# One score product ahead of a wait, and a reordered first batch, in a two-layer graph-attention kernel

## The chip, the cores and the metric

The kernel runs on one core of a Trainium2 chip. The metric is the device time of one execution in microseconds (us), and the number compared is the median of several executions. Before the change three executions took 3313.91, 3315.76 and 3318.42 us, so the median is 3315.76 us.

## The reference

The input is `x` with shape (16, 1024, 256) and an integer mask `adj` with shape (16, 1024, 1024). Two graph-attention layers follow each other, and each adds its result to `x`:

```
h = relu(layernorm(x))
# layer 0
n   = layernorm(h) * gamma1 + beta1               # 8 heads of width 32; q = k = v = n
h   = h + softmax(mask(n n^T / sqrt(32))) n
x   = x + h + gelu(layernorm(h)*gamma2+beta2 @ W1 + b1) @ W2 + b2
# layer 1
f   = relu(layernorm(x))
g   = f W
e   = leaky_relu(g a_1 (row) + g a_2 (column) + (g a_12) g^T, 0.2)
att = softmax(where(adj > 0, e, -9e15))
x   = x + elu(f W_1 + (att f) W_2)
```

The mask is symmetric. Batches do not depend on each other.

## The kernel before, in words

Everything is computed by `fast_path`; a second routine, `general_path`, is only entered when a check at the end says that the quick one is not accurate enough, and it does not run on these inputs. One batch has 1024 rows, which are cut into 8 tiles of 128 (`NT`), 4 chunks of 256 (`NCH`) or 2 halves of 512 (`NQH`).

The program is written out once by Python loops, without a loop on the chip. Six generators produce the pieces of work: `stream_a` (attention of layer 0), `stream_b` (the MLP and layer 1, called "rest"), `stream_p` (`prepare`, the second normalization), `stream_c` (`prologue`: load and normalize the next batch), `stream_m` (masks), `stream_s` (weights). Each yields a place on a common scale on which batch b's attention fills the stretch from b to b+1. The generator with the lowest place goes next. So the numbers in the `stream_...` functions decide the order in which instructions are issued. At the end the program adds an ordering dependency between successive instructions of each engine, so that every engine works strictly through its own list. A small list of deferred steps (`defer`) puts a step behind others by an estimated time; that too is only an order.

**Layer 0.** `attention` goes through units (half of the queries, group of four heads, key tile). In a unit, TensorE makes 4 score tiles (`s`, L1062), VectorE adds the mask to them (L1081), ScalarE takes the exponential (L1088), and in the unit after that TensorE weighs the values (`o`, L1183). In batch 0 there are 32 units; there TensorE adds the mask to half of the score tiles itself, by a product with an identity (`s<-mk,ident`, L574), and VectorE to the other half. In later batches VectorE adds every mask, and 8 of the 32 units are replaced by reading back weights from the other half (`mirror`, `weigh_mirrored`). The score tiles have one buffer each (`sc0`, `sc1`).

**The rest.** While batch b+1 is in its attention, TensorE also does the MLP (`ph`, `po`) and layer 1 of batch b. Layer 1 starts with a stage that this case is much about. `turn1(c)` turns the normalized features of chunk c into `fT` (`ptf`, L1423, copied out by ScalarE at L1426). `project_half(qh, oc)` makes half of `uT` (`puT`, copied out by ScalarE at L1438). `some_values(t, ...)` makes one tile `pg` of values each, copied to `gw` at L1453 by ScalarE for an even t and VectorE for an odd t. `some_weights(c, i)` makes the logits `lg` of chunk c against key tiles 2i and 2i+1; VectorE reads them twice (L1471), applies the leaky ReLU (L1476), and ScalarE takes the exponential (L1477). `ptf`, `puT`, `pg`, `lg`, `ph`, `po`, `pa`, `pf`, `ptk` and `ptos` share three PSUM buffers of one pool (`ps_tile`, `psm`); a product waits until an earlier tenant of its buffer has been read.

**The first batch.** `prologue` for b = 0 is written out by hand. Chunks 0 and 1 are normalized (`nrm`, L761), turned straight away (`turn_normed`, with gamma and beta applied by ScalarE during the copy to `kT`), and gamma and beta are applied to the values `va` by GpSimd (L863, L864). Chunks 2 and 3 go another way: GpSimd applies gamma and beta first (L844, L845), then `turn` transposes the result (`ptk`, L871).

**Masks.** `turn_masks(b, qh)` fetches the int32 mask in halves of a tile (two buffers, `adjp`), converts it on VectorE (`mq<-adj`, L594) and turns it by a transposing DMA. It runs in 5 pieces. `compare_masks(b, qh)` checks that the mask is symmetric: GpSimd subtracts (`odd`, L975), and the result is collected by ScalarE (a square with a sum, L985) for the first half and by VectorE (a maximum, L987) for the second. The tiles `odd` lie in a pool of six buffers.

Of the kernel before, what the change touches and what calls it, by code (L numbers as in the profile page):

```python
# [495 lines left out]
def fast_path(  # L496
# [307 lines left out]
    def prologue(b, st):  # L804
        h = hs[b] = [hp.tile([P, TPH, D], F32, tag=f"h{qh}", name=f"h{qh}_{b}") for qh in range(NQH)]


        va = st["va"] = vp.tile([P, NT, D], F32, tag="va", name=f"va_{b}")
        kT = st["kT"] = vp.tile([P, NG, N], F32, tag="kT", name=f"kT_{b}")
        stats = {}  # L810

        def load(i):
            ts = slice(i % 2 * TPC, (i % 2 + 1) * TPC)
            nc.sync.dma_start(
                h[i // 2][:, ts, :], x[b, i * CW : (i + 1) * CW, :].rearrange("(p r) d -> p r d", r=TPC)
            )

        def measure(i, which):
            stats[which, i] = norm_stats(
                [h[i // 2][:, i % 2 * TPC + j, :] for j in range(TPC)], f"{which}{b}_{i}"  # L820
            )

        def rectify(i):
            mv, rs = stats["a", i]
            nm = offset(mv, rs, f"{b}_{i}")
            for j in range(TPC):
                t = i * TPC + j
                nc.scalar.activation(
                    h[t // TPH][:, t % TPH, :],
                    h[t // TPH][:, t % TPH, :],  # L830
                    AF.Relu,
                    bias=nm[:, j : j + 1], scale=rs[:, j : j + 1]
                )

        def value(i):
            mv, rs = stats["b", i]
            for j in range(TPC):
                t = i * TPC + j
                nrm = tmpp.tile([P, D], F32, tag="w1", bufs=6, name=f"nrm_{b}_{t}")
                normalize(nrm, h[t // TPH][:, t % TPH, :], mv, rs, j)  # L840
                if b == 0 and i < 2:
                    normed[t] = nrm
                    continue
                nc.gpsimd.tensor_mul(nrm, nrm, g1)  # L844
                nc.gpsimd.tensor_add(va[:, t, :], nrm, be1)  # L845

        normed = {}

        def turn_normed(i):
            clock[0] += 0.5  # L850
            pt = ps_tile([P, NG, CW], f"ptk_{b}_{i}")
            for g in range(NG):
                for j in range(TPC):
                    nc.tensor.transpose(
                        pt[:, g, j * P : (j + 1) * P], normed[i * TPC + j][:, g * P : (g + 1) * P], ident
                    )
            for g in range(NG):
                nc.scalar.activation(
                    kT[:, g, i * CW : (i + 1) * CW], pt[:, g, :], AF.Identity, bias=be1c[:, g : g + 1], scale=g1c[:, g : g + 1]
                )  # L860
            for j in range(TPC):
                t = i * TPC + j
                nc.gpsimd.tensor_mul(va[:, t, :], normed[t], g1)  # L863
                nc.gpsimd.tensor_add(va[:, t, :], va[:, t, :], be1)  # L864

        def turn(i):
            clock[0] += 0.5
            pt = ps_tile([P, NG, CW], f"ptk_{b}_{i}")
            for g in range(NG):
                for j in range(TPC):  # L870
                    nc.tensor.transpose(  # L871
                        pt[:, g, j * P : (j + 1) * P], va[:, i * TPC + j, g * P : (g + 1) * P], ident
                    )
            nc.scalar.copy(kT[:, :, i * CW : (i + 1) * CW], pt)

        steps = [
            load,
            lambda i: None,
            lambda i: measure(i, "a"),
            rectify,  # L880
            lambda i: measure(i, "b"),
            value,
            lambda i: None,
            lambda i: turns.append((1, lambda: turn(i))),
        ]
        if b == 0:

            tiles = [midp.tile([P, 2, N], I32, tag=f"mid{i}", name=f"adj_0_{i}") for i in range(2)]
            adjs = [tiles[t // 2][:, t % 2] for t in range(TPH)]
            mqs = st["mq", 0] = mqp.tile([P, TPH, N], FP8, tag="mq", name="mq_0_0")  # L890
            m = st[0] = mkp.tile([P, NT // 2, QW, 2], FP8, tag="mk", name="mk_0_0")
            pairs = m.rearrange("p m q r -> p m (q r)").bitcast(BF16)

            def fetch(t):
                nc.sync.dma_start(adjs[t], rows(adj, 0, t))

            def convert(t):
                nc.vector.tensor_scalar(
                    mqs[:, t], adjs[t], 0.0, NEG8, op0=ALU.is_le, op1=ALU.mult, saturate=False
                )  # L900
                nc.sync.dma_start_transpose(pairs[:, :, t * P : (t + 1) * P], mqs[:, t].bitcast(BF16))

            load(0)
            load(1)
            for t in range(TPH):
                fetch(t)
                if t == 0:
                    for tile, src in first_rows:
                        nc.sync.dma_start(tile, src)
            load(2)  # L910
            load(3)
            measure(0, "a")
            measure(1, "a")
            rectify(0)
            rectify(1)
            measure(0, "b")
            measure(1, "b")
            value(0)
            turn_normed(0)
            convert(0)  # L920
            value(1)
            turn_normed(1)
            convert(1)
            convert(2)
            convert(3)
            yield
            for f in (lambda i: measure(i, "a"), rectify):
                for i in (2, 3):
                    f(i)
            yield  # L930
            measure(2, "b")
            value(2)
            yield
            measure(3, "b")
            value(3)
            yield
            for i in (2, 3):
                turns.append((1, lambda i=i: turn(i)))
                yield
            return  # L940
        for k in range(NCH + len(steps) - 1):
            for n in reversed(range(len(steps))):
                if 0 <= k - n < NCH:
                    steps[n](k - n)
                    yield
# [21 lines left out]
    def compare_masks(b, qh, st):  # L967

        for half in range(qh + 1):
            for i in range(TPH):  # L970
# [10 lines left out]
                n = (b * 3 + qh + half) * TPH + i  # L981

                def collect(odd=odd, n=n):
                    if qh == 0:
                        nc.scalar.activation(odd, odd, AF.Square, accum_out=uneven[:, n : n + 1])  # L985
                    else:
                        nc.vector.tensor_reduce(  # L987
                            uneven[:, n : n + 1], odd, axis=mybir.AxisListType.X, op=ALU.max, apply_absolute_value=True
                        )
# [332 lines left out]
    def rest(b, st, tails):  # L1322
# [262 lines left out]
        yield from some_values(2, 3)  # L1585
        if b == B - 1:
            ask(turn1, 3)
        yield from wait_for(turn1, 2)
        yield from some_values(4, 5)
        yield from some_weights(0, 0, 1)  # L1590
        yield from wait_for(turn1, 3)
        yield from project_half(1, 0)
        yield from project_half(1, 1)
        yield from some_values(6, 7)

# [38 lines left out]
        yield from spread(close_attention(), 4, B, B + .1)  # L1634

    def starts(b):
        return b + 0.99

    def stream_b():
        for b in range(B):  # L1640
# [22 lines left out]

    def stream_p():
        for b in range(B):
            place = starts(b) - 0.08
            yield place
            for c in range(2):
                while finished.get((b, 0), 0) < NG:
# [9 lines left out]
    def stream_c():  # L1679
        for b in range(B):  # L1680
            if b == 0:
                yield -0.6
                for place, _ in zip((0.005, 0.032, 0.034, 0.07, 0.10, 0.13), prologue(b, states[b])):
                    yield place
            else:
                yield from spread(prologue(b, states[b]), 32, b - 0.660, b - 0.150)

    def stream_m():
        for b in range(B):
            if b:  # L1690
                start, end = (b - 0.28, b - 0.10) if b == 1 else (b - 0.73, b - 0.60)
                yield from spread(turn_masks(b, 0, states[b]), 5, start, end)
                yield from spread(compare_masks(b, 0, states[b]), TPH, end + 0.05, end + 0.14)
                yield from spread(turn_masks(b, 1, states[b]), 5, b + 0.02, b + 0.16)
                yield from spread(compare_masks(b, 1, states[b]), 2 * TPH, b + 0.17, b + 0.26)
            else:
                yield from spread(compare_masks(b, 0, states[b]), TPH, b + 0.02, b + 0.2)
                yield from spread(turn_masks(b, 1, states[b]), 5, b + 0.23, b + 0.43)
                yield from spread(compare_masks(b, 1, states[b]), 2 * TPH, b + 0.52, b + 0.7)

    def stream_s():
        yield -0.3
# [82 lines left out]
```

## Time and profile before

| what | value |
|---|---|
| median of three executions | 3315.76 us |
| the profiled execution | 3309.42 us |
| its span | 3307.5 us |
| TensorE (PE) busy | 3216.8 us, 97% |
| VectorE (DVE) busy | 2575.4 us, 78% |
| ScalarE (ACT) busy | 2125.9 us, 64% |
| GpSimd (POOL) busy | 1660.3 us, 50% |
| DMA | 438.43 MB, mean 133 GB/s |

"Busy" counts the time in which an engine has an instruction in work; a busy TensorE is not TensorE at its peak. The profile also gives the share of its full clock that TensorE was granted in any stretch, the waits (who waited for whom, in total, how often, the longest), and a timeline of each engine. SP is the engine that issues the DMAs.

### The profile page before, as it was taken

What the parts mean: (1) busy time and instruction counts of PE and PEld (TensorE: products, weight loads), DVE (VectorE), ACT (ScalarE), POOL (GpSimd) and SP (SyncE); (2) the same over time, 40 slices, a digit from 0 to 9 for tenths busy, and PEclk for the clock granted to TensorE, in tenths of its full rate; (3) what the DMA queues carried; (4) which work ended last, traced back from release to release, by engine and by line L of the source; (5) the groups of instructions that cost most, each with busy time, mean ns of one, the idle gap of its engine ahead of it and who ended that gap; (6) DMA issues with size and microseconds to landing.
All of it is one profiled execution on the core that took longest, in us unless ns stands there. A gap on an engine that the chain in (4) does not pass through costs nothing. (4 is left out here: it accounts for less than half of the span.)

```text
span 3307.5 us, 115199 instructions
## 1 busy us (share of the span) xinstructions
PE 3216.8 (97%) x48642; PEld 1598.1 (48%) x48642; DVE 2575.4 (78%) x4568; ACT 2125.9 (64%) x5130; POOL 1660.3 (50%) x2397
## 2 busy tenths in 40 slices
PE   7799999999999999999999999999999999999998
PEld 2244445444454544445444454444545444454477
DVE  5688787888878888787888888888788787877734
ACT  6675665757667576675766657576675766757452
POOL 3565562735537365463645637365372654636120
PEclk9999999999999999999999999999999999999999
DMA  5264665646556465655646656465564746554410
GB/s 139 65 151 117 153 133 142 150 122 161 132 150 140 131 159 123 153 131 144 158 112 162 133 142 151 121 161 127 149 141 127 166 114 158 129 148 107 125 58 15
DMA packets 787789, 438.43 MB, mean 133 GB/s; under 512 B 178880, under 2 KB 738368, under 8 KB 787264
## 3 DMA queue, kind: packets, MB, share of 16 engines
q1 hardware_dynamic: 787264, 430.98, 53.4%
q8 instruction: 385, 6.31, 0.8%
q14 instruction: 140, 1.15, 0.1%
HBM read 250.75 MB, written 163.32 MB: 125 GB/s over the span
## 5 line engine op out<-in xcount | busy, mean ns | idle before, releaser
L1088 ACT ACTIVATE e<-e 128x512 f32<-128x512 f32 x1504 | 928.0, 618 | 502.0 <-DVE e L1081 498.0
L1081 DVE TENSOR_TENSOR e<-s,mk 128x1024 f32<-128x1024 f32 x748 | 878.2, 1214 | 127.3 <-PE s L1062 114.5
L574 PE MATMUL ph<-yT,w 128*32 128x256 f32 x7808 | 462.9, 382 | 15.1 <-DVE x L1104 6.0
L1183 PE MATMUL o<-e,va 128*32 128x512 f32 x3136 | 452.8, 611 | 7.9 <-ACT e L1088 7.9
L1062 PE MATMUL s<-kT 32*64 32x512 f32 x6272 | 455.6, 618 | 3.9 <-DVE e L1081 3.0
L574 PE MATMUL lg<-fT,uT 128*32 128x256 f32 x7680 | 450.1, 379 | 0.0
L574 PE MATMUL pa<-gw,e 128*32 128x258 f32 x7584 | 446.0, 380 | 0.0
L574 PE MATMUL po<-w,hid 128*32 128x256 f32 x7680 | 434.8, 379 | 0.4 <-ACT hid L1382 0.4
L574 PEld LDWEIGHTS ph<-yT,w 128*32 128x32 f32 x7808 | 269.7, 110 | 205.4 <-issue 28.2
L574 PEld LDWEIGHTS po<-w,hid 128*32 128x32 f32 x7680 | 251.9, 110 | 201.8 <-issue 43.3
L574 PEld LDWEIGHTS lg<-fT,uT 128*32 128x32 f32 x7680 | 248.6, 110 | 197.9 <-issue 27.2
L574 PEld LDWEIGHTS pa<-gw,e 128*32 128x32 f32 x7584 | 246.1, 110 | 185.4 <-issue 22.1
L1117 POOL TENSOR_TENSOR part<-part,x 128x512 f32<-128x512 f32 x240 | 310.9, 1295 | 18.8
L1104 DVE STREAM_TRANSPOSE x<-e 128x1024 f32<-128x1024 f32 x240 | 290.7, 1226 | 33.2 <-ACT e L1088 27.2
L1088 ACT ACTIVATION_READ_ACCUMULATOR e<-e 128x1 f32 x1504 | 281.3, 187 | 0.0
L1471 DVE SCALAR_TENSOR_TENSOR e<-lg,gw,mk 128x256 f32<-128x256 f32 x512 | 222.1, 475 | 69.9 <-PE lg L574 60.9
L1477 ACT ACTIVATE e<-e,shift 128x512 f32<-128x512 f32 x256 | 183.1, 716 | 137.1 <-DVE e L1476 125.5
L844 POOL TENSOR_TENSOR nrm<-nrm,g 128x256 f32<-128x256 f32 x124 | 97.1, 783 | 307.3 <-DVE nrm L761 307.3
L1183 PEld LDWEIGHTS o<-e,va 128*32 128x32 f32 x3136 | 69.3, 108 | 351.9 <-issue 212.0
L1378 ACT ACTIVATE hid<-ph,b1c 128x256 f32<-128x256 f32 x512 | 202.2, 464 | 57.2 <-PE ph L574 42.0
L975 POOL TENSOR_TENSOR odd<-mk,mq 128x512 bf16<-128x512 fp8e5 x192 | 219.4, 1161 | 0.0
L1117 POOL TENSOR_TENSOR part<-x 128x512 f32<-128x512 f32 x120 | 155.8, 1298 | 114.8 <-DVE x L1104 114.7
(158 smaller groups left out, 4396.6 us busy)
## 6 DMA issues: line engine op xcount, KB each, us to landing
blocks<-x SPq DMA_DIRECT2D x480, 256.0 KB, 4.7
em<-blocks SPq DMA_DIRECT2D x240, 512.0 KB, 4.2
adj<-in_adj_dram SPq DMA_DIRECT2D x248, 256.0 KB, 3.7
h<-in_x_dram SPq DMA_DIRECT2D x64, 256.0 KB, 4.4
xb<-in_x_dram SPq DMA_DIRECT2D x128, 128.0 KB, 3.2
turned<-yT SPq DMA_DIRECT2D x64, 256.0 KB, 3.3
yT<-turned SPq DMA_DIRECT2D x256, 64.0 KB, 2.0
out_dram<-z SPq DMA_DIRECT2D x128, 128.0 KB, 3.9
```

Of the source, the lines that this page charges most:

```text
L574: nc.tensor.matmul(out[c : c + HD], lhsT[:, c : c + HD], rhs, start=start, stop=stop)
L844: nc.gpsimd.tensor_mul(nrm, nrm, g1)
L975: nc.gpsimd.tensor_tensor(odd.rearrange("p (u v x) -> p u v x", u=2, v=2), key.rearrange("p (u v x) -> p u v x", u=2, v=2), query.rearrang ...
L1062: nc.tensor.matmul(sc[j // 2][c : c + P // 2, j % 2, :], kT[r, g, kt * P + c : kt * P + c + P // 2], kT[r, g, qs], start=j >= by_pe, stop= ...
L1081: nc.vector.tensor_tensor(e, masked, mask.unsqueeze(1).to_broadcast([P, 2, QW]), op=ALU.add)
L1088: nc.scalar.activation(e[:, j], masked[:, j], AF.Exp, scale=SCALE, accum_out=sums[kt // TPH, g][:, n, kt % TPH, qh : qh + 1],)
L1104: nc.vector.transpose(x[:, :, 2 * i : 2 * i + 2, :].rearrange("p c h j -> p h c j"), es[i].rearrange("p h (c i) -> p h c i", i=HD),)
L1117: add = lambda out, p, q: nc.gpsimd.tensor_tensor(out, p, q, op=ALU.add)
L1183: nc.tensor.matmul(o[j * HD : (j + 1) * HD, :], va[:, kt, (g * GH + j) * HD : (g * GH + j + 1) * HD], es[j // 2][:, j % 2, :], start=first ...
L1378: nc.scalar.activation(hid[:, f0 + i, :], ph[:, i, :], AF.Identity, bias=b1c[:, f0 + i : f0 + i + 1])
L1471: nc.vector.scalar_tensor_tensor(e[:, j, :], lg[:, j, :], gw[:, kt, D : D + 1], st[c // 2][:, kt // 2, qs, kt % 2], op0=ALU.add, op1=ALU.add,)
L1477: ready = defer(2.5, lambda: nc.scalar.activation(e, e, AF.Exp, bias=shift))
```

## The change

There are five edits.

1. In layer 1 of every batch, the logits of chunk 0 against key tiles 0 and 1 are made ahead of `wait_for(turn1, 2)` and values 4 and 5, and those against key tiles 2 and 3 between the two halves of the second projection.
2. In batch 0, chunks 2 and 3 are normalized as chunks 0 and 1 are: `nrm` is turned directly, ScalarE applies gamma and beta in two activations for each chunk, and GpSimd makes `va` from `nrm` in a step of its own (`scale_values`), outside the transposition. The steps of both chunks stand in another order.
3. The collecting step of the symmetry check goes from ScalarE to VectorE for the first half of the masks in batches 0 and 1.
4. Places in `stream_m`: in batch 0, four comparisons begin later and eight stand in the stretch 0.45 to 0.54 where it was 0.52 to 0.70; both halves of batch 1's masks are fetched and converted earlier, all within batch 0's attention.
5. The MLP of batch 0 starts at 1.03 instead of 0.99, `prepare` keeps its place.

```diff
@@ prologue
-                if b == 0 and i < 2:
+                if b == 0:
                     normed[t] = nrm
                     continue
@@ turn_normed
+        def scale_values(i):
             for j in range(TPC):
                 t = i * TPC + j
                 nc.gpsimd.tensor_mul(va[:, t, :], normed[t], g1)
                 nc.gpsimd.tensor_add(va[:, t, :], va[:, t, :], be1)
@@ prologue, b == 0
             value(1)
             turn_normed(1)
-            convert(1)
-            convert(2)
-            convert(3)
+            for t in range(1, TPH):
+                convert(t)
+            scale_values(0)
+            scale_values(1)
             yield
-            for f in (lambda i: measure(i, "a"), rectify):
-                for i in (2, 3):
-                    f(i)
+            for i in range(2, NCH):
+                measure(i, "a")
             yield
-            measure(2, "b")
-            value(2)
+            for i in range(2, NCH):
+                rectify(i)
+            for i in range(2, NCH):
+                measure(i, "b")
+            for i in range(2, NCH):
+                value(i)
             yield
-            measure(3, "b")
-            value(3)
+            turns.append((1, lambda: turn_normed(2)))
+            scale_values(2)
             yield
-            for i in (2, 3):
-                turns.append((1, lambda i=i: turn(i)))
-                yield
+            turns.append((1, lambda: turn_normed(3)))
+            scale_values(3)
             return
@@ compare_masks
-                    if qh == 0:
+                    if qh == 0 and b > 1:
                         nc.scalar.activation(odd, odd, AF.Square, accum_out=uneven[:, n : n + 1])
@@ rest
+        yield from some_weights(0, 0)
         yield from wait_for(turn1, 2)
         yield from some_values(4, 5)
-        yield from some_weights(0, 0, 1)
         yield from wait_for(turn1, 3)
         yield from project_half(1, 0)
+        yield from some_weights(0, 1)
         yield from project_half(1, 1)
         yield from some_values(6, 7)
@@ starts, stream_p
-        return b + 0.99
+        return b + (0.99 if b else 1.03)
-            place = starts(b) - 0.08
+            place = b + 0.91
@@ stream_c
-                for place, _ in zip((0.005, 0.032, 0.034, 0.07, 0.10, 0.13), prologue(b, states[b])):
+                for place, _ in zip((0.005, 0.032, 0.07, 0.10, 0.13), prologue(b, states[b])):
@@ stream_m
-                start, end = (b - 0.28, b - 0.10) if b == 1 else (b - 0.73, b - 0.60)
+                start, end = (b - 0.44, b - 0.30) if b == 1 else (b - 0.73, b - 0.60)
                 ...
-                yield from spread(turn_masks(b, 1, states[b]), 5, b + 0.02, b + 0.16)
+                start, end = (b - 0.16, b - 0.03) if b == 1 else (b + 0.02, b + 0.16)
+                yield from spread(turn_masks(b, 1, states[b]), 5, start, end)
                 ...
-                yield from spread(compare_masks(b, 0, states[b]), TPH, b + 0.02, b + 0.2)
+                yield from spread(compare_masks(b, 0, states[b]), TPH, b + 0.10, b + 0.20)
                 yield from spread(turn_masks(b, 1, states[b]), 5, b + 0.23, b + 0.43)
-                yield from spread(compare_masks(b, 1, states[b]), 2 * TPH, b + 0.52, b + 0.7)
+                yield from spread(compare_masks(b, 1, states[b]), 2 * TPH, b + 0.45, b + 0.54)
```

## The prediction

> **What bounds the kernel now.** I read the page first: the table of engines, then the slices of PE.
>
> ```profile
> PE 3216.8 (97%) x48642; PEld 1598.1 (48%) x48642; DVE 2575.4 (78%) x4568; ACT 2125.9 (64%) x5130; POOL 1660.3 (50%) x2397
> PE   7799999999999999999999999999999999999998
> ```
>
> TensorE (PE) is busy 97% of the span, so what shortens the run is idle time of PE, PE at less than its full clock, or PE work removed. No edit removes a matmul. The 7s say that the idle time sits in the first two slices, some 165 us. The busy time by stretches says more (columns: stretch and length, busy PE, PEld, DVE, ACT, POOL with counts, the granted clock of PE, DMA share, GB/s):
>
> ```profile
> 60.00:95.00 35.00, 31.26 (x455) 9.25 (x449) 21.12 (x42) 28.17 (x90) 10.88 (x20) 0.97 0.32 88
> 95.00:115.00 20.00, 13.38 (x134) 3.34 (x132) 13.74 (x23) 12.48 (x37) 13.89 (x22) 0.83 0.00 1
> 115.00:145.00 30.00, 25.94 (x291) 6.92 (x276) 19.95 (x38) 22.63 (x70) 15.66 (x23) 1.00 0.35 89
> 145.00:185.00 40.00, 31.62 (x380) 15.91 (x380) 24.07 (x35) 26.98 (x66) 18.77 (x24) 0.87 0.55 136
> 1200.00:3080.00 1880.00, 1855.25 (x29220) 902.83 (x29216) 1523.62 (x2649) 1234.19 (x2967) 1003.94 (x1430) 1.00 0.57 139
> ```
>
> PE idles 6.6 us in 95 to 115 and 8.4 in 145 to 185, both also below full clock. In the steady stage it idles 25 us in 1880, about 2.7 for each batch of some 200 us; DVE is 81% busy there, so it is the next to become late. Which waits these are, the list of PE's waits tells (total us, times, longest):
>
> ```profile
> PE s L574 <- ACT e L1088: 17.0, 18, 4.4
> ...
> PE pg L574 <- ACT gw L1453: 10.9, 14, 0.9
> PE pg L574 <- ACT uT L1438: 10.8, 15, 1.0
> ...
> PE ph L574 <- DVE x L1104: 6.0, 1, 6.0
> ...
> PE s L1062 <- DVE e L1081: 3.0, 4, 2.0
> ```
>
> The two `pg` rows come once in nearly every batch. The `L574 <- L1438` row is the one that edit 1 touches; one instance, from the timeline of PE:
>
> ```profile
> 1068.09 3.62 PE L574 MATMUL puT<-fT,wm 128*32 128x512 f32 x32
> 1071.53 1.05 PE L574 MATMUL pg<-wo,fT 128*32 128x258 f32 x16
> 1073.38 1.08 PE L574 MATMUL pg<-wo,fT 128*32 128x258 f32 x16 [0.81 <-ACT uT L1438]
> ```
>
> Two halves of `puT` and values 6 go into the three PSUM buffers back to back; values 7 need a fourth and wait until ScalarE has copied the first `puT`, behind four exponentials and an L1477. The other, `<- gw`, lies earlier, at values 3.
>
> **What the Trainium skill says.** "Perfetto Trace Analysis", Optimization Strategy: a gap that comes back regularly on an otherwise full engine can mean too few buffers. The 15 waits of 0.7 us agree. "TensorE: Matmul & The Clock Gate", Part 1: The HAM clock gate: PE falls to half clock after a window, some 3.4 us, without enough work. The trace agrees: its low-clock stretches at 58.7, 150.8 and 174.7 last 3.4, 6.9 and 3.4 us, 99.6 lasts 6.9, and eight `s` matmul groups take 2.01 there against 1.11.
>
> **The change part by part.** All on the profiled execution (3309.42 us, span 3307.5), which is 6.3 under the median of the three; I carry the shift over. A measurement can tell about 0.2%, here 6.6 us, from no change.
>
> *Edit 1, 16 batches.* Same instructions, another order. Before: `pg_4`, `pg_5`, both products `lg_0_0` and `lg_0_1`, a score unit, the two halves of `puT`, `pg_6`, `pg_7`, so that nothing lies between the first `puT` and the values but the second. After, by buffers: `lg_0_0`, `pg_4`, `pg_5`, first `puT`, a score unit, `lg_0_1`, second `puT`, `pg_6`, `pg_7`. Now `pg_6` waits for the copy of the first `puT`, which has the unit (1.11+1.06), `lg_0_1` (1.83) and the second `puT` (1.85) to finish in: 5.8 us, with ScalarE done some 4 us early. `pg_7` waits for DVE's second L1471 of `lg_0_1` (pair 0.87 us): by the timeline DVE is done near 1071.6, needed at 1073.1, 1.5 to spare. The first `puT` waits for L1471 of `lg_0_0`, 0.8 to spare. So 15 waits go: **−10.8**. The `gw` wait at `pg_3` is ahead of all this and stays (0). What comes with it: DVE gets two pairs of L1471 at other moments, and is up to 1.5 us later at the next unit's mask additions (1.23 each); with 81% busy it catches up within a few units, and the two steps between `s` and its use hide it. If not, see the rivals.
>
> *Edits 2, 3, 4 up to 71 us.* The rectifying of chunks 2 and 3 (two pairs of 1.08 on ScalarE) leaves its place ahead of unit 1's exponentials, for which PE waits 2.3 us at 25.7; the two activations more for each chunk cost 2×0.45 on ScalarE twice. Net **−1.3**.
>
> *71 to 114 us.* Before, a comparison on POOL (1.15) stands ahead of `nm` and ScalarE's rectifying ahead of the exponentials:
>
> ```profile
> 96.39 1.15 POOL L975 TENSOR_TENSOR odd<-mk,mq 128x512 bf16<-128x512 fp8e5 x1
> 98.17 1.09 ACT L828 ACTIVATE h<-h,nm,rs_a 128x256 f32<-128x256 f32 x2 [3.17 <-POOL nm L770]
> 100.46 1.04 PE L574 MATMUL s<-mk,ident 128*32 128x512 fp8e5 x8 [4.36 <-ACT e L1088]
> ```
>
> After: that 4.36, 1.8 more near it, and the half clock from 99.6 (half of 6.9, 3.4) go: −9.6. Against that, the burst of comparisons on POOL (1.15 each) now stands ahead of the `nm` of batch 1's second chunk: rectifying 2 us later, PE idle 2.9. Eight comparisons' reduces (0.68 on DVE against 0.7 on ScalarE; four here) and the mask conversions of batch 1's first half stand in DVE's queue ahead of mask additions. A piece's second half comes 4.0 to 5.3 us after the first, since the two `adj` buffers are refilled by a DMA issued on SP after the conversion; a unit lasts 3.07 us, so a piece in each unit stretches it to some 4.5: about 6 units by 1.4, so 8.1. Sum 2.9+8.1−9.6: **+1.4**.
>
> *114 to 145 us.* The second half's conversions (DVE, 0.43 each, waits of 3.3) now lie in four units of batch 0, ahead of their additions: the last exponentials come 1.65 later. A transposition waits for `va` on POOL behind two comparisons (+0.9), a reduce fewer on DVE (−0.4). **+2.1**.
>
> *145 to 183 us, and edit 5.* `ph` waits 6.0 for L1104 at 151.8 and keeps its place behind it: not gained. But the conversions that held up batch 1's additions are gone:
>
> ```profile
> 169.85 0.43 DVE L594 TENSOR_SCALAR mq<-adj 128x512 fp8e5<-128x512 int32 x1 [3.26 <-DMA adj<-in_adj_dram]
> 172.18 2.22 PE L1062 MATMUL s<-kT 32*64 32x512 f32 x16 [2.00 <-DVE e L1081]
> ```
>
> With that 2.0, 1.1 beside it and half of the half-clock stretch at 174.7 (1.7) go: −4.8; PE has one unit less between two score steps while the MLP is later, +0.3. **−4.5**. Later MLP work is the same, only later; the list of PE from batch 2 on differs by edit 1 alone. The DMAs that a moved piece issues (two loads of half a tile and a transposing one on SP for each) move with it, ahead of what batch 0 issues on SP between 75 and 145 us; that is next to nothing, as `DMA share` is 0.00 to 0.35 there, and their cost is in the stretched units above. POOL gets `scale_values` in place of the same multiplications inside the transposition: no work more.
>
> Sum: −1.3+1.4+2.1−4.5 = −2.3 in the first batch, −10.8 after: −13.1. Profile 3296.3, median 3315.8−13.1 = **3302.7**.
>
> The first batch is not shown by the old trace. Bounds: without any low clock in 71 to 183, and with the conversions hidden, it gives −12; the other end is rival D. I take the sum of the steps.
>
> **The rivals.**
> *A. Opening better than summed.* Conversions fit between additions (DVE is 60% busy in 60 to 95): −12−10.8 gives 3293.
> *B. The `pg` wait changes its releaser.* If DVE is 1.5+0.7 us later than I think at `lg_0_1`, `pg_7` waits as long for L1471 as it did for L1438. Only −2.3: 3313.5. For it: DVE at 81%. Against: DVE has few waits of its own there.
> *C. Slower: the early logits hold a buffer.* `puT` behind `lg_0_0` has only 0.8 us to spare. If DVE, behind mask additions of 1.23, reads it two additions (2.5) later, PE waits 1.7 in each of 15 batches in place of 0.7: +15−2.3, 3328. It decides from a lateness of 1.5 us, where the wait equals the old one. Against it: with an order fixed on every engine, the additions ahead of L1471 are the same few in every batch, and I find them done in time.
> *D. The opening falls to half clock.* In units of 4.5 us with 2.6 of PE work PE is 58% busy, with holes of 1.9. If windows fail, a unit costs 1.5 more: 12 units, +18 on the sum, 3320.7. For it: the old trace lost its clock in 95 to 115, where PE was 67% busy. Against: at half clock PE is busier, and comes back.
>
> **How the numbers follow.** Forecast 0.62 (3295 to 3310), A 0.12, B 0.08, C 0.07, D 0.11. Faster by 0.2% (under 3309.1): forecast without its tail, 0.59, and A: 0.71. Within: B, that tail, half of D: 0.16. Slower: C, half of D: 0.13. Range: 3290 to 3318 leaves out C, half of D and a little of A.
>
> **What would show it.** In the profile after: the row `pg <- uT` gone and no row of `pg` or `puT` waiting for L1471 above 2 us in all; PE idle in a steady batch down from 2.7 to 2.0; no 4.4 in `s <- e` and no 2.0 in `s <- L1081`; the wait of 6.0 on L1104 still there; full clock at 100 and 175. Wrong would be: a row of 10 us for L1471, or a clock under 0.9 in 71 to 145.

## The result, and the profile after

Ten executions of the changed kernel took 3322.06 to 3329.51 us, median 3325.41; ten of the kernel before, 3316.07. The ratio is 1.0029, interval 1.002 to 1.0037: slower by 9.3 us, where 13 less was forecast. It lies outside the range. The profiled execution of the change took 3328.74 us, 3.3 above its median, that of before 3309.42, 6.7 below; so the two traces differ by 19.3 us, and half of that is which executions were profiled. Experiments below are read by their ratios; a thousandth is 3.3 us.

In the changed kernel the lines behind the first-batch code stand four further: L1081 is now L1085, L1088 L1092, L1165 L1169, L1192 L1196, L1453 L1457, L1476 L1480. First the stretches of the changed kernel (columns as in the prediction):

```profile
60.00:95.00 35.00, 29.69 (x434) 8.64 (x427) 22.70 (x41) 27.64 (x87) 14.49 (x22) 0.98 0.34 88
95.00:115.00 20.00, 16.05 (x128) 3.76 (x127) 13.91 (x29) 11.48 (x35) 11.59 (x19) 0.85 0.52 132
115.00:145.00 30.00, 26.35 (x272) 7.14 (x268) 19.80 (x39) 20.99 (x63) 15.44 (x20) 0.93 0.20 51
145.00:185.00 40.00, 33.14 (x419) 14.48 (x423) 23.90 (x32) 25.69 (x65) 19.65 (x28) 0.96 0.49 117
185.00:400.00 215.00, 201.74 (x3081) 99.26 (x3079) 159.54 (x292) 130.61 (x314) 102.82 (x149) 0.96 0.51 126
1200.00:3080.00 1880.00, 1854.69 (x29228) 906.22 (x29224) 1530.71 (x2654) 1240.74 (x2974) 1018.77 (x1438) 1.00 0.57 140
```

The stretch from 185 to 400 of the kernel before, for which the prediction has no term:

```profile
185.00:400.00 215.00, 210.74 (x3344) 104.65 (x3328) 176.54 (x314) 141.15 (x339) 117.17 (x166) 1.00 0.59 141
```

There the time was lost: PE idles 13.3 us in place of 4.3, at 0.96 of its clock in place of 1.00, and gets 263 matmuls less done. The steady stage, where 10.8 us were to be won, has PE busy for the same time as before (1854.7 and 1855.3 of 1880). VectorE is busier there, 1530.7 against 1523.6. The waits of PE after:

```profile
PE s L574 <- ACT e L1092: 11.5, 16, 2.5
PE pg L574 <- ACT gw L1457: 10.6, 13, 1.1
PE o L1169 <- DVE os L1196: 8.7, 13, 1.0
...
PE lg L574 <- ACT gw L1457: 6.4, 1, 6.4
...
PE lg L574 <- ACT uT L1442: 2.6, 1, 2.6
PE ptf L1427 <- ACT hid L1382: 2.4, 1, 2.4
```

The row `pg <- uT` of 10.8 us is gone, as forecast; no row of `pg` or `puT` waiting for VectorE came. In its place stands one that was not there, `o <- os` with 8.7 us, once in nearly every batch. The three single waits of 6.4, 2.6 and 2.4 us all lie between 229 and 291 us. The largest is best read in the order of time (start, duration, engine, line; then what it waited for):

```profile
280.08 1.28 POOL L1121 TENSOR_TENSOR part<-x 128x512 f32<-128x512 f32 x1
281.44 2.64 POOL L1121 TENSOR_TENSOR part<-part,x 128x512 f32<-128x512 f32 x2
284.16 1.21 POOL L1121 TENSOR_TENSOR part<-part 128x256 f32<-128x256 f32 x2
285.45 0.72 POOL L1121 TENSOR_TENSOR row<-part 128x64 f32<-128x64 f32 x1
286.26 0.24 POOL L769 TENSOR_SCALAR nm<-mv_a 128x2 f32<-128x2 f32 x1
...
286.81 1.09 ACT L828 ACTIVATE h<-h,nm,rs_a 128x256 f32<-128x256 f32 x2 [6.50 <-POOL nm L770]
...
290.25 0.35 ACT L1457 COPY gw<-pg 128x257 f32<-128x257 f32 x1
290.66 3.64 PE L574 MATMUL lg<-fT,uT 128*32 128x256 f32 x32 [6.40 <-ACT gw L1457]
```

GpSimd adds up a row of blocks (L1121, 6 us) before it makes the small `nm` for chunk 2 of batch 2. ScalarE's rectifying waits 6.5 us for `nm`, and in ScalarE's queue four exponentials and the copy of values 6 stand behind the rectifying. PE needs that copy and waits. By the trace's record of the clock PE is then at half clock from 286.4 to 296.6: its next products of 32 take 3.64 us where they took 1.91. Before, `nm` stood ahead of this chain:

```profile
274.91 0.24 POOL L769 TENSOR_SCALAR nm<-mv_a 128x2 f32<-128x2 f32 x1
...
275.38 1.27 POOL L1117 TENSOR_TENSOR part<-x 128x512 f32<-128x512 f32 x1
```

This is the mechanism that the prediction had seen at 98 us, POOL ahead of ScalarE's rectifying, at another place.

### The profile page after: what moved, and what is told of

Same layout as the page of the kernel before. It is cut to its first block, busy times and chain, and to the rows that moved or that the text cites. A ratio compares the mean times of both kernels' runs of the same rounds, so it can differ in the third digit from the quotient of the medians.

```text
span 3327.0 us, 115163 instructions
## 1 busy us (share of the span) xinstructions
PE 3229.6 (97%) x48642; PEld 1603.4 (48%) x48642; DVE 2588.4 (78%) x4576; ACT 2125.3 (64%) x5116; POOL 1676.2 (50%) x2397
## 3 DMA queue, kind: packets, MB, share of 16 engines
q14 instruction: 139, 1.14, 0.1%
## 5 line engine op out<-in xcount | busy, mean ns | idle before, releaser
L1092 ACT ACTIVATE e<-e 128x512 f32<-128x512 f32 x1504 | 928.4, 619 | 493.1 <-DVE e L1085 487.2
L1085 DVE TENSOR_TENSOR e<-s,mk 128x1024 f32<-128x1024 f32 x748 | 878.2, 1213 | 138.0 <-PE s L1066 122.1
L1066 PE MATMUL s<-kT 32*64 32x512 f32 x6272 | 464.9, 622 | 3.8 <-DVE e L1085 2.9
L1121 POOL TENSOR_TENSOR part<-part,x 128x512 f32<-128x512 f32 x240 | 311.0, 1296 | 18.8
L1092 ACT ACTIVATION_READ_ACCUMULATOR e<-e 128x1 f32 x1504 | 282.7, 188 | 0.0
L1480 DVE SCALAR_TENSOR_TENSOR e<-e 128x512 f32<-128x512 f32 x256 | 213.3, 833 | 8.8
```

The lines of the kernel that those rows point to most:

```text
L1066: nc.tensor.matmul(sc[j // 2][c : c + P // 2, j % 2, :], kT[r, g, kt * P + c : kt * P + c + P // 2], kT[r, g, qs], start=j >= by_pe, stop= ...
L1085: nc.vector.tensor_tensor(e, masked, mask.unsqueeze(1).to_broadcast([P, 2, QW]), op=ALU.add)
L1092: nc.scalar.activation(e[:, j], masked[:, j], AF.Exp, scale=SCALE, accum_out=sums[kt // TPH, g][:, n, kt % TPH, qh : qh + 1],)
L1121: add = lambda out, p, q: nc.gpsimd.tensor_tensor(out, p, q, op=ALU.add)
L1480: nc.vector.scalar_tensor_tensor(e, e, ALPHA, e, op0=ALU.mult, op1=ALU.max)
```

## The experiments

Each was timed side by side with the kernel before, and ratio and interval are against that.

**Which edit moved the chain, and what edit 1 brings.** Edit 1 alone, on the kernel before:

```diff
+        yield from some_weights(0, 0)
         yield from wait_for(turn1, 2)
         yield from some_values(4, 5)
-        yield from some_weights(0, 0, 1)
         yield from wait_for(turn1, 3)
         yield from project_half(1, 0)
+        yield from some_weights(0, 1)
         yield from project_half(1, 1)
```

> The kernel before with edit 1 alone. Theory (VectorE is full at this place and takes the gain back): the row pg <- uT (10.8 us) is gone and a row o L1165-line <- os copy of 8 to 9 us stands in its place, time 3314 to 3316 against 3316. Rival (my forecast; the loss lies all in the first batches): 3305, that is 10.8 less, and no such row. The trace from 320 us on should then run parallel to that of the changed kernel in both.

Ratio 0.9986 (0.9977 to 0.9994): 4.6 us less, between the two expectations. In this kernel the lines keep their old numbers up to L1580. Its waits (who waited for whom: total, times, longest):

```profile
PE pg L574 <- ACT gw L1453: 11.1, 14, 0.9
PE o L1165 <- DVE os L1192: 8.7, 14, 0.7
```

10.8 us of one wait went and 8.7 of another came. So edit 1 is a small gain, and no part of the slowdown.

Edit 5 alone:

```diff
-        return b + 0.99
+        return b + (0.99 if b else 1.03)
 ...
-            place = starts(b) - 0.08
+            place = b + 0.91
```

> The kernel before with edit 5 alone (the MLP of batch 0 starts at 1.03). Theory (edit 5 moves a chain of GpSimd additions ahead of the normalization of batch 2 and makes the rest of batch 0 denser): 12 to 17 us slower, 3328 to 3333, with a wait of about 6 us of ScalarE's rectifying for nm and half clock near 290 us. Rival (the other edits' places cost the time): 3315 to 3317.

Ratio 1.0066 (1.0053 to 1.008): 22 us slower, more than either expected. Two places in its trace stand out. At 172.6 us PE waits 6.8 us for VectorE's additions: the masks of batch 1 are converted at their old places, two conversions ahead of the additions had waited 7.4 us for a transfer, and the MLP that filled PE there before now comes later. The changed kernel has no such wait. At 297.5 PE waits 3.7 us, and there it is `nm` behind the chain again, as expected: ScalarE's rectifying waits 8.6 us for it, and 6.8 us of half clock go with it. So edit 4 seems to take back a part of what edit 5 costs; that is read from the trace, and no run has edits 4 and 5 alone.

The changed kernel with the old start again:

```diff
-        return b + (0.99 if b else 1.03)
+        return b + 0.99
```

> The changed kernel with edit 5 undone (the MLP of batch 0 starts at 0.99 again, edits 1 to 4 kept). Theory: the 16 us between 235 and 305 us are gone, the rest stays, 3309 to 3313. Rival (edits 2 to 4 or 1 bring the loss): 3322 to 3327.

Ratio 0.9991 (0.9982 to 0.9999): 3 us less than before. So edit 5 is the loss, about 12.6 us in the company of the others (1.0029 − 0.9991; some 4 us either way by the two intervals).

**How edit 5 loses it.** The changed kernel, with only the place of the two instructions of one `nm` on GpSimd changed:

```diff
-            defer(6.5, add_up)
+            defer(8.5 if (b, g, kt) == (1, 1, 7) else 6.5, add_up)
```

> The changed kernel with one chain of GpSimd additions (part, the last of group 1 in batch 1) put behind one nm of batch 2 in GpSimd's list; nothing else differs. Theory: the wait of 6.4 us (lg <- gw) goes, and with it most of the 10.2 us of half clock: 8 to 11 us less, 3314 to 3317. Rival (the dense rest, not this order, holds PE up): another wait comes in its place, 0 to 3 us less, 3322 to 3325.

Ratio 1.0011 (1.0005 to 1.0018), median 3316.8. In GpSimd's list these two instructions are the only ones that moved, and the lists of VectorE and ScalarE are the same as in the changed kernel. `lg <- gw` falls from 6.4 to 0.3 us and the half clock at 286 is gone. So two small instructions behind a chain of additions cost 6 us by the ratios, less than the 8 to 11 expected, and about half of what edit 5 lost. (The medians differ by 8.6, but the kernel before was 2.1 us quicker beside this run than beside the changed kernel.) The waits of 2.6 and 2.4 us stay, each with a stretch of 3.4 us at half clock.

For the other half the code of the stream has a hint: the rest of a batch is spread over the distance of two starts, and with 1.03 that distance falls to 0.96 for batch 0.

```diff
-            start, length = starts(b), starts(b + 1) - starts(b)
+            start, length = starts(b), 1.0
```

> The changed kernel, where the rest of batch 0 still starts at 1.03 but is spread over a length of 1.0 in place of 0.96. The chain of GpSimd stands behind nm again, as in the run with one chain later (3316.8). If the rest being 4% denser made what that run had left over (5.5 us above the run without edit 5): 3310 to 3312. If the start one unit later made it: 3315 to 3319, with the two waits of 2.4 and 2.6 us (ptf <- hid, lg <- uT) still there.

Ratio 0.9992 (0.9984 to 1.0). Still one unit later, but not squeezed, the rest costs nothing: both waits are gone (one `puT <- fT` of 2.9 came) and the clock stays full from 225 to 320 us, where its mean was 0.91 in the changed kernel. So the start at 1.03 is harmless; that the end did not move with it is what cost. The spacing shifts several steps at once (the chain is behind `nm` here too), so the second half is shown to come from the squeeze, but is not pinned on one step.

**Why edit 1 brings 4 and not 11.** VectorE in edit 1 alone, batch 5, where the timeline shows no pause from 1067.1 to 1087.4:

```profile
1077.87 0.85 DVE L1471 SCALAR_TENSOR_TENSOR e<-lg,gw,mk 128x256 f32<-128x256 f32 x2
1078.76 1.69 DVE L1476 SCALAR_TENSOR_TENSOR e<-e 128x512 f32<-128x512 f32 x1
...
1084.46 2.35 DVE L1081 TENSOR_TENSOR e<-s,mk 128x1024 f32<-128x1024 f32 x2
1086.72 0.68 DVE L1192 COPY os<-o 128x512 f32<-128x512 f32 x1
```

PE in the same kernel, at the first product that reads weights back:

```profile
1087.46 0.64 PE L1165 MATMUL o<-em,va 128*32 128x256 f32 x8 [0.62 <-DVE os L1192]
```

The same copy and the same product in the kernel before, without a wait:

```profile
1086.54 0.68 DVE L1192 COPY os<-o 128x512 f32<-128x512 f32 x1
1087.89 0.61 PE L1165 MATMUL o<-em,va 128*32 128x256 f32 x8
```

The PSUM pool of `o` has one buffer, so this product waits until VectorE has copied the sum before it. Relative to the before trace PE came 1.2 us earlier to the block of three `lg` (1075.08, before 1076.32), but VectorE made the copy at the same moment (1086.72, before 1086.54). So the next run keeps edit 1 and relieves VectorE there: the copies of values 5 and 7 go to ScalarE.

```diff
-            (nc.vector.tensor_copy if t % 2 else nc.scalar.copy)(gw[:, t, : D + 1], pg[:, : D + 1])
+            (nc.vector.tensor_copy if t in (1, 3) else nc.scalar.copy)(gw[:, t, : D + 1], pg[:, : D + 1])
```

> The kernel before with edit 1, and the copies gw of values 5 and 7 go from VectorE to ScalarE. Theory (VectorE, without a pause from the score additions to the os copy, sets when the first read-back product may start): the copy of values 7, 0.39 us, leaves that stretch, the wait o <- os falls from 0.62 to some 0.25 a batch, 15 times 0.39 = 6 us less than edit 1 alone: 3304. Rival (it is ScalarE or the order of PE): o <- os stays at 8 to 9 us or ScalarE's copies become a wait, 3309 to 3314.

Ratio 0.9951 (0.9937 to 0.9964): 16 us less than before, about 12 more than edit 1 alone where 6 was expected. `o <- os` is down to 0.4 us in all. VectorE after that:

```profile
1077.01 0.69 DVE L1476 SCALAR_TENSOR_TENSOR e<-e 128x512 f32<-128x512 f32 x1
...
1083.98 0.68 DVE L1192 COPY os<-o 128x512 f32<-128x512 f32 x1
```

The same L1476 takes 0.69 in place of 1.69. In edit 1 alone it starts in the middle of two additions of GpSimd's:

```profile
1077.26 2.64 POOL L1117 TENSOR_TENSOR part<-part,x 128x512 f32<-128x512 f32 x2
```

The Trainium skill says in "SBUF — State Buffer", section "SBUF: two separate sides", that VectorE and GpSimd share a pair of ports as an exclusive lock, and that an instruction of VectorE with two inputs in SBUF takes part in it against a GpSimd instruction that reads SBUF: who starts first holds it, the other waits. L1476 is of that kind, and the traces agree closely. Alone it takes 0.69 us. In the fourteen traces 825 of 3584 L1476 (L1480 in the changed kernels) take over 0.8 us; each of them began inside a GpSimd instruction, and its time is what was left of that one plus 0.54 to 0.56 us. Here: GpSimd's second addition ends at 1079.90, 1.14 us after L1476 began, and 1.14 + 0.55 is 1.69. With the copies moved L1476 comes first, and it is GpSimd that waits: the same two additions take 3.02 us in place of 2.64. In one point the measurement differs from the page, which has the pair held for the whole instruction: beside GpSimd's L757 (128x2, 0.71 us, reads SBUF too) L1476 was not held up in any of the 642 cases that had over 0.2 us of it left.

The 256 L1476 of a run take 201.7 us before, 213.2 with edit 1, 202.7 with the copies moved as well. So 11.5 us more of VectorE came with edit 1 in a stretch where it had none to spare, and a copy of 0.39 taken out ahead of L1476 won both.

The same copies without edit 1:

> The kernel before with the same two copies on ScalarE and nothing else. Theory (before, ScalarE ends the wait of pg and VectorE has 0.7 us to spare at the os copy, so that VectorE's time is worth nothing): within 3 us of the kernel before. Rival (any relief of VectorE counts): 6 us less.

Ratio 0.9996 (0.9987 to 1.0004): nothing. `pg <- uT` is still there with 11.1 us. Neither of the two alone is worth much; together they are worth 16 us.

Half of edit 1:

```diff
         yield from some_values(4, 5)
-        yield from some_weights(0, 0, 1)
+        yield from some_weights(0, 0)
         yield from wait_for(turn1, 3)
         yield from project_half(1, 0)
+        yield from some_weights(0, 1)
         yield from project_half(1, 1)
```

> The kernel before with half of edit 1: the logits lg_0_1 go between the halves of the projection, lg_0_0 stays behind values 5. The row pg <- uT goes as with the whole edit. If VectorE loses time because the leaky ReLU of lg_0_0 (L1476) comes to lie beside GpSimd's multiplications, this half keeps VectorE earlier and o <- os stays under 5 us: 3303 to 3307. If any order that starts the projection sooner meets VectorE's own work: o <- os 8 to 10 us, 3308 to 3312 as with the whole edit.

Ratio 0.9992 (0.9983 to 1.0), `o <- os` 8.5 us. My guess that the place of `lg_0_0` makes the collision falls: with `lg_0_0` at its old place the L1476 take even more, 217.8 us. Both orders that start the projection sooner meet VectorE.

**The first batch.** Edits 2, 3 and 4 alone (the changed kernel with the diff of edit 1 and that of the start taken back):

> The changed kernel without edits 1 and 5: only edits 2, 3 and 4, all in the first batch and the masks of the second. My forecast of them: 2.3 us less than before. Theory now: nothing clear of noise, between 3 less and 3 more. Rival (they bring a loss of their own that edit 1 hides in the run without edit 5): 4 to 6 us more.

Ratio 1.0006 (0.9997 to 1.0014): no clear difference.

**Better versions.** The changed kernel without edit 5, with the copies of 5 and 7 on ScalarE:

> The changed kernel without edit 5, with the two copies on ScalarE: edits 1 to 4 and the relief of VectorE. Theory: 6 us less than without the relief, 3305. Rival: 3310 to 3312, as without.

Ratio 0.9957 (0.9944 to 0.9971), median 3301.15: 14 us less than before and about 11 less than without the copies, where 6 was expected; no better than edit 1 with the copies.

On the kernel before, edit 1, with three copies on VectorE:

```diff
-            (nc.vector.tensor_copy if t % 2 else nc.scalar.copy)(gw[:, t, : D + 1], pg[:, : D + 1])
+            (nc.vector.tensor_copy if t in (0, 1, 3) else nc.scalar.copy)(gw[:, t, : D + 1], pg[:, : D + 1])
```

> The kernel before with edit 1, the copies of values 5 and 7 on ScalarE, and the copy of values 0 on VectorE. Theory: the other regular wait, pg <- gw (11.7 us, values 3 behind ScalarE's copy of values 0), goes too, as VectorE makes that copy 3 us sooner and has 0.8 us of pause there: 8 to 11 us less than without, 3287 to 3291. Rival (as with edit 1, the wait passes to the next resource): 3296 to 3300.

Ratio 0.9934 (0.9921 to 0.9948), median 3290.69: the fastest here. Its waits:

```profile
PE ptf L1423 <- ACT uT L1438: 2.7, 9, 0.3
...
PE o L1165 <- DVE os L1192: 0.4, 1, 0.4
```

`pg <- gw`, 11.7 us in the run with the copies of 5 and 7 moved, is gone; what took its place is 0.3 us at a time, and PE idles 15.3 us in 1200 to 3080 where it idled 20.8. So here a wait went and did not only change its name. It fits that VectorE, which took the work, had a pause there (0.76 us ahead of its copy of values 3 in the run with two copies moved). By the ratios the step is worth 5.6 us of the 8 to 11 expected, and the two intervals overlap.

The same copies with half of edit 1:

> The kernel before with half of edit 1 and the copies of the run before this one. Theory: within 3 us of that run, since with VectorE relieved the place of lg_0_0 does not matter; rival: 3 to 8 us more, if a wait of lg_0_1 or values 7 comes back.

Ratio 0.9944 (0.993 to 0.9958), 4 us above by the medians; the intervals overlap, so it stays open whether the place of `lg_0_0` matters there.

## Why the prediction was wrong, step by step

- **Edit 1, "So 15 waits go: −10.8": the waits went, the time did not.** All followed from the PSUM buffers, and of them no row came back, as forecast. The step that failed is the next one, "with 81% busy it catches up within a few units, and the two steps between `s` and its use hide it". 81% is a mean over the batch. In the 20 us that end with the `os` copy VectorE has no pause at all, and there PE meets it again. Measured: −4.6 us (−2.0 to −7.6), with 8.7 of the 10.8 us in another row. PE's idle time in the steady stage stayed at 2.7 us a batch, where 2.0 was forecast. Rivals B and C had the right engine and the wrong place: they looked for the lateness at `pg_7` and the first `puT`, 15 us and more too soon.
- **Edit 5, "Later MLP work is the same, only later": this failed, and it set the sign.** The +0.3 for it should have been about +12. The list of instructions was compared from batch 2 on, and the stages of the sum end at 183 us; batch 1, where the rest of batch 0 runs, was in neither. The rest was not only later but squeezed into 0.96, and GpSimd's list had two instructions behind a chain of 6 us.
- **The first batch up to 183 us, −2.3: near the measured value by luck.** The addition that lies at 177.1 us before starts 1.9 us earlier after. But 19 products `ph` fewer have been made by then (153, before 172): at 1.91 us for 32 that is an estimated 1.1 us of PE's work which edit 5 only puts off, and up to 185 us PE makes the same number of products in both (1619 and 1620). The steps between are off too: at 147.5 the addition is 5.7 late where the steps gave 2.2, and the three traces that have edits 2 to 4 without edit 5 are 5 us late at 177.1. The 4.4 of `s <- e` is down to 2.5, as forecast, and the wait of 6.0 us of `ph` is still there, 5.9, now put down to a transfer; but the half clock near 100 is 3.4 us and not gone, and more came (10.2 us from 27.0, 3.4 at 112 and at 129). A part of that is which execution was profiled: half clock near 25 us, 3.4 to 6.8 of it, is in all seven other traces with the old opening and only not in that of the kernel before. Alone, edits 2 to 4 are worth nothing clear of noise, +2 us.
- **Rival D**, half clock through the opening, did not decide: the clock was 0.98, 0.85 and 0.93 in the three stretches, 0.93 on the mean, and the loss lies later.

Slips in the prediction's working change the sum by less than 1 us: 6 units by 1.4 are 8.4 us, not 8.1; 2.3 less 2×0.45 is 1.4, not 1.3, and 0.5 if the 0.45 are counted twice; the 2.01 us given for eight score groups are those of one group of 16.

The parts do not simply add up. Alone, edit 1 measures −4.6, edits 2 to 4 +2 and edit 5 +22 us, together 19; the change as a whole is 9.3 slower. Edits 1 to 4 together are worth −3, close to their parts, so it is edit 5 that costs some 9 us less in the company of the others.

## What to carry to other kernels

A wait of the full engine can be removed only up to the next place where it meets another engine's queue: follow that queue, instruction by instruction, from the wait to the next meeting, and trust its pauses there, not its mean load. Where a planner places work by a scale, a moved start also changes the distance to the next start; compare the lists of all engines in every batch that the moved work reaches, small instructions on the slow engine first. And an edit that only uncovers the next limit may be worth most together with one that is worth nothing alone.

## What was not expected of the hardware

The same VectorE instruction (128x512, two inputs in SBUF) takes 0.69 us alone, and 1.69 where it starts inside an addition of GpSimd's: it ends 0.55 us after GpSimd's does. A shift of 0.39 us in its queue decides between the two. Around a wait of 6.4 us TensorE was at half clock for 10.2 us, from 286.4 on, though it was nearly always busy from 290.7. The length of a wait alone did not decide this: after waits of 2.4 and 2.6 us the changed kernel ran 3.4 us at half clock (from 231.8 and 266.0), while after one of 2.9 us, at 256.4 in the run that is late but not denser, the clock stayed full.
